# Mixture weights loaded in one head and parted in the next, every other head from 7 to 42

## The chip, the core and the metric

The kernel runs on one core of a Trainium2 chip. The core has five engines with instruction queues of their own: PE (TensorE, matrix products), DVE (VectorE), ACT (ScalarE), POOL (GpSimd) and SP (SyncE, which here issues nearly all the DMAs). [...] The metric is the device time of one execution in microseconds (us), lower is better, as the median of several runs.

## The reference, cut to what matters

One transformer block over 4 sequences of 512 tokens, 256 wide, all in float32: causal attention with 16 heads, and then a mixture of 8 experts of which each token uses two.

```python
mod = (_silu(c) @ wmod).reshape(B, 6, 1, -1)
sa, ca, ga, sb, cb, gb = (mod[:, i] for i in range(6))
...
h = _layernorm(x) * (1 + ca) + sa
x = x + ga * attention(h, W_K, W_Q, W_V, W_O)
h = _layernorm(x) * (1 + cb) + sb
x = x + gb * mixture(h, ...)
```

```python
# mixture, x being h above
h = x @ down_w + down_b
gate, topi = softmax_of_top_2(softmax(x @ router_w + router_b - COST_LAMBDA * cost))
for k in range(2):
    mask = one_hot(topi[..., k], 8)
    for e, (w1, b1, w2, b2) in enumerate(expert_params):
        hm = h * mask[..., e:e + 1]
        acc = acc + (gelu(gelu(hm) @ w1 + b1) @ w2 + b2)
    out = out + acc * gate[..., k:k + 1]
out = out + 0.1 * (gelu(gelu(h) @ shared_w1 + shared_b1) @ shared_w2 + shared_b2)
out = out @ up_w + up_b + gelu(x) @ core_w + core_b
```

The experts' hidden widths are 128, 256, 384, 512, twice. The change concerns the weights of this mixture, but its instructions run in the middle of the attention.

## The kernel before, in words

**Products in three parts.** To keep float32 accuracy at a fast matmul, most operands are *parted*: `hi` is the operand cast to `float32r`, `lo` is what is left (`full - hi`), and a product is three matmuls (`mm3`, lines 139 to 141). Activations are parted as they come out of PSUM: a cast on ACT and a subtraction (`rest`, line 147).

**Mixture weights are parted early and kept in DRAM.** `UNITS` cuts the mixture's weights into units of up to four blocks of 128 columns. Eleven are to be parted, in this order (`TO_PART`): first0 to first4, second0 to second2, shared, core, down; all have 128x512 elements but shared and down, which have 128x256. `part_wf` (line 218) does one unit:

- load the unit from `wf` into a `stage` tile `st_wf` (line 181, one DMA for each run of adjacent blocks, so one to three),
- for the second units, write the whole unit to DRAM (line 225),
- cast it to `hi_wf` on ACT, which takes another `stage` tile (line 227), and write that to DRAM (line 228),
- subtract on POOL, in place in `st_wf` (line 147), and write that to DRAM (line 230).

There are two buffers of the tag `stage`. They are also used by `load_unit` (line 184) for the attention's weights `wqk`, `wv`, `wo`, and by `route`. The parted units come back from DRAM with `load_wf` and `load_parts` near the end of the attention.

**The loop over heads.** The attention runs over 64 heads, numbered n = 0 to 63 (four groups of four heads, in each group the four sequences). One turn of the loop holds, for head n: the scores `ps` in four tiles t = 0 to 3 (line 475 for t = 0, `mm3` for the others), a reduction on DVE that leaves the scores in `e` and their least in `nmax` (line 481), the exponential on ACT (line 491), the reciprocal of the sum on DVE (line 495) and the scaling on POOL (line 496). Between them stand the projections `pq` and `pk` of head n + 1 and half of the values `pv` of a pair of heads. Then `turned` transposes `e` in blocks on DVE into `T` (lines 505 and 511), writes `T` to DRAM in four DMAs (`moved`, line 517) and reads it back as `aT` (line 521). `parted` casts `aT` on ACT to `aTh` (line 528) and subtracts on POOL. Three heads later `mixed` multiplies it with the values into `pz`, which ACT casts into `zh` (line 546) and DVE parts into `zl`, and one turn later `project_out` multiplies that with `wo` into `po`. The tiles `e`, `T`, `aTh` and the PSUM tile of the scores have two buffers each, `aT` three.

**What sets the order.** TensorE's instructions stay in the order of the code (`manual_schedule`). Those of the other engines and of SP are put in order by the framework's planner[...]. [...] Some attention weights must wait: the tag `wu` has ten buffers, so that in each group the loads from the second `wqk` of head 12 (28, 44) on wait for weights to fall out of use.

`PART_AT` (line 101) lists the heads in whose turn a unit is parted; lines 1042 and 1043 call `part_wf` there, ahead of the projections of that turn:

```python
PART_AT = (17, 19, *range(20, 28), 33)
...
        if n in PART_AT:
            part_wf(TO_PART[PART_AT.index(n)])
```

## Time and profile before

| | |
|---|---|
| median of 3 runs | 824.99 us (823.43 to 825.74) |
| the profiled execution | 824.06 us |
| its span | 822.3 us |
| TensorE busy | 777.1 us (95%), mean granted clock 0.988 |
| VectorE busy | 597.4 us (73%) |
| ScalarE busy | 490.4 us (60%) |
| GpSimd busy | 521.4 us (63%) |
| DMA moved | 124.12 MB, mean 151 GB/s |
| attention on TensorE, from the first score of head 0 to that of head 63 | 19.73 to 625.63 us |

The profile is of one execution. An engine's busy time is the sum of its instructions; waiting is not in it. In the timeline each line has a start, a length, the engine, the line of the kernel, the operation, out<-in with tile names, and in brackets how long the engine had been idle before it and what released it. A matmul's end is modelled. SPq is the DMA-issuing queue: its records show the issue, not the transfer; from issue to landing a load of 256 KB takes between 3 and 4 us in the median (`st_wqk` 3.8, `st_wv` 3.4), the 160 KB of one `moved` 2.8 and the 640 KB of an `aT` 3.9 us.

### The profile page before, as it was taken

How to read it: one execution, taken by the hardware profiler on the slowest of the kernel's cores; microseconds unless marked ns; L12 is line 12 of the kernel's file. 1: busy time of each engine (PE TensorE's matmuls, PEld its weight loads, DVE VectorE, ACT ScalarE, POOL GpSimd, SP SyncE). 2: the span in 40 equal slices, each digit the busy share in tenths (PEclk: the TensorE clock that was granted, in tenths of full speed). 3: DMA queues.
4: the chain of work that ended last, by engine and by line, in shares of the span. 5: the costliest groups of instructions: out<-in, count | busy, mean ns of one | idle time of the engine just before them, and what ended most of it. 6: DMA issues, size and time to landing. Idle time of an engine off the chain costs nothing. (4 is left out here: it accounts for less than half of the span.)

```text
span 822.3 us, 14105 instructions
## 1 busy us (share of the span) xinstructions
PE 777.1 (95%) x4487; PEld 671.3 (82%) x4487; DVE 597.4 (73%) x1734; ACT 490.4 (60%) x1184; POOL 521.4 (63%) x523
## 2 busy tenths in 40 slices
PE   6889999999998799999999999999998898989997
PEld 5678989999887689999999999999887775767775
DVE  5968787776655676767777776779898577795555
ACT  3556666566656656666666656665667343656663
POOL 4645566886756568866556895656565346564675
PEclk9999999999999999999999999999999899999999
DMA  7365354666676746665454665554566332222221
GB/s 235 113 182 156 111 151 128 198 174 204 200 212 198 218 151 183 188 179 161 128 156 133 198 168 162 165 157 138 155 182 216 104 120 86 94 62 68 61 81 61
DMA packets 73218, 124.12 MB, mean 151 GB/s; under 512 B 8996, under 2 KB 51252, under 8 KB 73144
## 3 DMA queue, kind: packets, MB, share of 16 engines
q1 hardware_dynamic: 73112, 123.21, 51.1%
q8 instruction: 36, 0.59, 0.3%
q14 instruction: 38, 0.31, 0.1%
q0 software_dynamic: 32, 0.02, 0.0%
HBM read 73.05 MB, written 50.14 MB: 150 GB/s over the span
## 5 line engine op out<-in xcount | busy, mean ns | idle before, releaser
L147 POOL TENSOR_TENSOR aT<-aT,aTh 128x1152 fp32r<-128x1152 f32 x64 | 171.9, 2687 | 127.1 <-ACT aTh L528 124.2
L496 POOL TENSOR_SCALAR e<-e,inv 128x128 f32<-128x128 f32 (+3 forms) x256 | 135.7, 543 | 66.8 <-DVE inv L495 64.8
L491 ACT ACTIVATE e<-e,nmax 128x128 f32<-128x128 f32 (+3 forms) x256 | 143.4, 562 | 45.9 <-DVE nmax L481 44.8
L528 ACT CAST aTh<-aT 128x1152 fp32r<-128x1152 f32 x64 | 74.0, 1156 | 127.4 <-DMA aT<-moved 64.5
L481 DVE CUSTOM_DVE_ANT_0 e<-ps,mask 128x128 f32<-128x128 f32 (+3 forms) x256 | 120.9, 479 | 31.0 <-PE ps L475 19.7
L511 DVE STREAM_TRANSPOSE T<-e 128x384 f32<-128x384 f32 (+2 forms) x256 | 100.4, 445 | 9.8 <-POOL e L496 9.7
L139 PE MATMUL ps<-kh,ql 128*128 128x256 f32 (+2 forms) x192 | 72.0, 375 | 17.1 <-DVE nmax L481 17.1
L147 DVE TENSOR_TENSOR zl<-pz,zh 128x512 fp32r<-128x512 f32 x64 | 44.0, 687 | 56.9 <-ACT zh L546 56.3
L139 PE MATMUL po<-wo,zl 128*128 128x256 f32 x256 | 73.3, 286 | 4.5 <-DVE zl L147 4.2
L140 PE MATMUL po<-wo,zh 128*128 128x256 f32 x256 | 72.0, 281 | 0.0
L141 PE MATMUL po<-wo,zh 128*128 128x256 f32 x256 | 72.0, 281 | 0.0
L139 PE MATMUL pv<-wv,hTl 128*128 128x256 f32 x256 | 71.7, 280 | 0.0
L140 PE MATMUL pv<-wv,hTh 128*128 128x256 f32 x256 | 71.5, 279 | 0.0
L141 PE MATMUL pv<-wv,hTh 128*128 128x256 f32 x256 | 71.5, 279 | 0.0
L856 POOL TENSOR_TENSOR oacc<-oacc,part 128x512 f32<-128x512 f32 x28 | 40.9, 1462 | 43.4 <-DVE part L852 36.8
L495 DVE RECIPROCAL inv<-tot 128x1 f32<-128x1 f32 x256 | 40.0, 157 | 36.5 <-ACT e L491 29.6
L139 PE MATMUL pz<-aTh,vl 128*128 128x512 f32 (+2 forms) x192 | 65.5, 341 | 0.0
L140 PE MATMUL pz<-aT,vh 128*128 128x512 f32 (+2 forms) x192 | 65.3, 340 | 0.0
L140 PE MATMUL ps<-kl,qh 128*128 128x256 f32 (+2 forms) x192 | 65.2, 339 | 0.2 <-DVE kl L147 0.2
L141 PE MATMUL pz<-aTh,vh 128*128 128x512 f32 (+2 forms) x192 | 65.3, 340 | 0.0
L141 PE MATMUL ps<-kh,qh 128*128 128x256 f32 (+2 forms) x192 | 64.9, 338 | 0.0
L139 PEld LDWEIGHTS ps<-kh,ql 128*128 128x128 f32 x192 | 36.6, 191 | 28.0 <-DVE nmax L481 19.9
(216 smaller groups left out, 2331.2 us busy)
## 6 DMA issues: line engine op xcount, KB each, us to landing
moved<-T SPq DMA_DIRECT2D x256, 160.0 KB, 2.8
aT<-moved SPq DMA_DIRECT2D x64, 640.0 KB, 3.9
spread<-gates_e SPq DMA_DIRECT2D x32, 256.0 KB, 3.2
st_wqk<-in_wqk SPq DMA_DIRECT2D x16, 256.0 KB, 3.8
wf_first<-wfp_first SPq DMA_DIRECT2D x5, 512.0 KB, 5.9
st_wv<-in_wv SPq DMA_DIRECT2D x8, 256.0 KB, 3.4
st_wo<-in_wo SPq DMA_DIRECT2D x8, 256.0 KB, 3.7
wmod<-in_wmod SPq DMA_DIRECT2D x6, 256.0 KB, 5.2
```

The lines of the kernel that those rows point to most:

```text
L139: nc.tensor.matmul(o, lhsT=wl, rhs=mh, start=start, stop=False)
L140: nc.tensor.matmul(o, lhsT=wh, rhs=ml, start=False, stop=False)
L141: nc.tensor.matmul(o, lhsT=wh, rhs=mh, start=False, stop=stop)
L147: return eng.tensor_tensor(lo, full, f32(hi), ALU.subtract)
L481: least = nc.vector.tensor_tensor_reduce(out=et, in0=ps[:, :n], in1=maskf[:, S - n :], scale=-SCALE, scalar=BIG, op0=ALU.add, op1=ALU.min, ...
L491: exp = nc.scalar.activation(et, et, AF.Exp, bias=nm[:, t : t + 1], scale=-1.0, accum_out=tot[:, t : t + 1])
L495: nc.vector.reciprocal(inv[:, one], tot[:, one])
L496: by_sum = nc.gpsimd.tensor_scalar(et, et, inv[:, one], 1.0, ALU.mult, ALU.mult)
L511: nc.vector.transpose(to[:, first : first + n], blocks[:, at : at + (n - 1) * step + 1 : step])
L528: nc.scalar.copy(hi, full)
L856: recent["added"] = nc.gpsimd.tensor_tensor(oacc, oacc, to, ALU.add).ins
```

## The change

The load is taken out of `part_wf` into a function of its own, `stage_wf`, which is called one head ahead of `part_wf`; and the eleven heads are others: 7, 9, 11, then 20, 22, 24, 26, then 36, 38, 40, 42. The order of the units is the same. The loads are thus called in heads 6, 8, 10, 19, 21, 23, 25, 35, 37, 39 and 41.

```diff
-PART_AT = (17, 19, *range(20, 28), 33)
+PART_AT = (7, 9, 11, 20, 22, 24, 26, 36, 38, 40, 42)
...
+    staged: dict[str, bass.AP] = {}
+
+    def stage_wf(u: str):
+        n = len(UNITS[u][0]) * P
+        staged[u] = work.tile([P, 512], F32, tag="stage", name=f"st_wf_{u}")[:, :n]
+        load_runs(staged[u], wf_runs(u))
+
     def part_wf(u: str):
 
         n = len(UNITS[u][0]) * P
-        st = work.tile([P, 512], F32, tag="stage", name=f"st_wf_{u}")[:, :n]
-        load_runs(st, wf_runs(u))
+        st = staged[u]
         d = parts_d[u] = dram.tile([P, 3, n], F32, tag=f"wfp_{u}", name=f"wfp_{u}")
         if u.startswith("second"):
             nc.sync.dma_start(d[:, 2, :], st)
...
         for f, *args in later.pop(n, ()):
             f(*args)
+        if n + 1 in PART_AT:
+            stage_wf(TO_PART[PART_AT.index(n + 1)])
         if n in PART_AT:
             part_wf(TO_PART[PART_AT.index(n)])
```

## The prediction, made before the changed kernel was run

> **What bounds the kernel now.** The order of reading was: the page's busy table and its 40 slices, then the same in windows cut at heads, then who waits for whom in the bad stretch, then the timeline there. TensorE is busy 777.1 of 822.3 us, so the question is where the other 45 us lie. In the page's slices (20.6 us each) these two rows answer it:

> ```profile
> PE   6889999999998799999999999999998898989997
> ...
> PEclk9999999999999999999999999999999899999999
> ```

> Outside the start, the attention half (slices 0 to 30) has one hole, slices 11 to 13. A head begins on TensorE with its first score product (line 475); the timeline has these at 137.58 (head 12), 211.10 (head 20) and 309.10 (head 29). Heads 12 to 19 take 9.19 us each, and so do the heads from 29 on. Heads 20 to 28 take 98.00 us where nine of 9.19 us are 82.7: **15.3 us are lost there**, and since everything behind moves at TensorE's pace, they are lost to the end. The windows of heads 7, 21, 23 and 26 (columns: from and to, length, then busy us of PE, PEld, DVE, ACT, POOL with counts, clock, DMA share, GB/s):

> ```profile
> 90.60:99.78 9.18, 9.18 (x60) 8.38 (x59) 7.30 (x23) 5.81 (x15) 6.06 (x6) 1.00 0.53 145
> ...
> 220.54:231.53 10.99, 9.44 (x61) 8.31 (x59) 6.04 (x21) 7.12 (x19) 6.62 (x6) 1.00 0.66 215
> ...
> 241.63:254.78 13.15, 9.72 (x60) 8.38 (x59) 6.02 (x22) 6.44 (x17) 5.99 (x7) 1.00 0.69 201
> ...
> 276.98:289.58 12.60, 9.45 (x60) 8.31 (x59) 8.72 (x28) 7.78 (x20) 6.69 (x7) 1.00 0.69 226
> ```

> No engine is full in the long heads (ACT 6 to 8 us of 11 to 13); something waits. The waits between 205 and 300 us name it (us in total, times, longest):

> ```profile
> ACT hi_wf_second L227 <- DMA st_wf_second<-in_wf: 11.2, 2, 6.0
> ...
> ACT hi_wf_first L227 <- DMA st_wf_first<-in_wf: 5.1, 2, 2.6
> ACT hi_wf_shared L227 <- DMA st_wf_shared<-in_wf: 3.7, 1, 3.7
> ...
> ACT hi_wf_core L227 <- DMA st_wf_core<-in_wf: 2.2, 1, 2.2
> ```

> That is 22.2 us in which ScalarE stood before the cast of a mixture unit whose load had not landed. The timeline around 248 us shows how it reaches TensorE:

> ```profile
> 243.49 1.44 SPq L181 DMA_DIRECT2D st_wf_second<-in_wf  x3
> ...
> 248.50 0.33 SPq L225 DMA_DIRECT2D wfp_second<-st_wf_second  x1
> 248.53 0.62 ACT L227 CAST hi_wf_second<-st_wf_second 128x512 fp32r<-128x512 f32 x1 [5.98 <-DMA st_wf_second<-in_wf]
> ...
> 248.87 2.20 SPq L517 DMA_DIRECT2D moved<-T  x4
> 249.05 1.15 ACT L528 CAST aTh<-aT 128x1152 fp32r<-128x1152 f32 x1
> ...
> 250.72 0.69 DVE L147 TENSOR_TENSOR zl<-pz,zh 128x512 fp32r<-128x512 f32 x1 [5.46 <-ACT zh L546]
> ...
> 251.46 0.39 PE L139 MATMUL po<-wo,zl 128*128 128x256 f32 x1 [2.23 <-DVE zl L147]
> ```

> Two queues stand: ScalarE behind the cast (aTh, zh and the exponentials are late, then VectorE, then TensorE), and SP behind line 225, which waits for the same load, so that `moved` is issued late and with it the next `aT`. With one unit in every head the loads leave SP at 231.56, 243.49, 254.97 and 266.55: a loop of some 11.6 us in a head of 9.19.

> [...] `moved` leaves at 248.87, right behind line 225. [...] here three issues took 1.44 us and their landing 4.3 us median. [...] heads 2 and 3 (35.55 to 57.31) ran at a clock of 0.84 and 0.85, with 128x512 matmuls of 0.63 us instead of 0.39.

> **The change, part by part.** Nothing is added or removed: the eleven units keep their loads, casts (0.62 us, 0.41 for two blocks), subtractions on POOL (1.29, 0.75) and writes; TensorE's list is instruction for instruction the same, and the other engines' lists have the same lengths. What moves is read from the order of each engine's instructions in both programs. The planner lifts work ahead as buffers allow, so the places are not those of the code. Before: first0 and first1 are cast at the starts of heads 17 and 19, then eight units follow in heads 19 to 25, one or more per head, then down at head 33. After, three groups:
> - A: first0, first1, first2 in heads 2, 3 and 4 (the code says 7, 9, 11).
> - B: first3 at the start of head 19, first4, second0, second1 at the ends of heads 19, 20, 21.
> - C: second2 at the start of head 35, shared, core, down up to the start of head 37.

> *Removed, the run of eight: 15.3 us.* Head 28 (10.33 us) counts as its tail, since head 12, of the same kind, takes 9.19. When this stall goes, nothing else is late there: TensorE itself needs the 9.19 us, so no more than 15.3 can be had.

> *B.* first3 stands as first1 did, loaded two heads ahead: nothing (first1's cast at 205.25 waited for nothing). first4 stands as first2 did, whose ScalarE wait of 2.48 us cost head 20 only 0.25 us. second0: SP issues its load behind `moved` of head 19, at about 217 instead of 231.6, and `aT` goes out between the load and line 225, so the landing (4.3 us) overlaps work that has to wait anyway; ScalarE, there at about 219, waits until about 221.5, 2.5 us. But the cast now stands behind vh of its head, not ahead of it as first3's did at 221.16, where vl (2.97 us) and the 1.55 us of TensorE at 224.22 followed. second1's load leaves at about 225.5 and lands by 230; ScalarE gets there at about 230.5. So 0.25 + some 1 + some 0.75: **2 us**. Low end 0.5 (first4 alone costs); high end 5.7, three times the mean of the old run (15.3/8 = 1.9).

> *C.* second2 is loaded two heads ahead: nothing. shared stands as first2 did. core's load waits on SP for a stage buffer ahead of `moved` of head 35, so that and its `aT` leave 1 to 2 us later than in B. down stands as down did before, which cost nothing (head 33 took 9.19). **1.5 us**; low 0, high 4 (two units at 1.9).

> *A.* On SP the load of first0 stands behind `moved` of head 0, at 36.7; a load issued at 36.77 landed in 3.9, so 40.6. ScalarE is at the cast at 38.4 and waits 2.2 us. The load of first1 goes half behind `moved` of head 1, which itself comes 1.6 us later (behind first0's writes and the four gate rows): landing about 51.5, ScalarE there at 50.6, wait 0.9. first2: landing about 59.3, ScalarE there at 58.1, wait 1.2. These 4.3 us have cover, because in this stretch ScalarE waits for `aT` in each head:

> ```profile
> 44.75 1.16 ACT L528 CAST aTh<-aT 128x1152 fp32r<-128x1152 f32 x1 [2.18 <-DMA aT<-moved]
> ...
> 61.59 1.16 ACT L528 CAST aTh<-aT 128x1152 fp32r<-128x1152 f32 x1 [3.50 <-DMA aT<-moved]
> ```

> On POOL 3 x 1.29 us stand ahead of softmax scalings, and POOL is busy 2.76 and 6.76 us of heads 2 and 3. VectorE's list puts the transposes of heads 1, 3 and 4 behind a score reduction they preceded, which takes away waits like the 1.48 us of TensorE at 60.91. Taken at **0.5 us**. From below: a gain of 1.5. From above: all 4.3 us uncovered plus one more half-clock window (3.4 us long, as the two at 38.5 and 48.5, so 1.7 lost): 6.

> Sum: 15.3 - 2 - 1.5 - 0.5 = 11.3 us. The profiled execution took 824.06 us (span 822.3): 812.8. The median of the three runs is 0.9 above that execution, which gives 813.7; I say **813 us**.

> **The rivals.**
> - *The stall is only moved.* The planner leaves groups B and C one unit per head, so the change isn't the spacing it says. If each of their six close units costs the old 1.9 us, 11.5 come back: gain 3.8, less 0.5, **821**. For it: casts still follow their load closely in SP's list. Against: the loss grew along the old run (0.25, 1.8, 0.9, 4.0 us in heads 20 to 23), and runs of three end before it grows.
> - *No change.* Groups B and C at their high ends (9.7) and A near its own (6): **824.5**. Against: three independent groups would all have to go badly.
> - *The start pays: slower.* Heads 2 to 4[...] half clock holds from 37 to 68 us, 31 us lose 15.5, of which 3.4 (two windows) are lost already: 12.1, and 4.3 of waits: 16.4. Net 16.4 + 3.5 - 15.3 = 4.6 slower, **829**. It decides from a loss of 11.8 us in the start. For it: the clock of 0.84. Against: [...] the cover above.

> **How the numbers follow.** Forecast 0.73; moved stall 0.13; no change 0.05; start pays 0.09. A measurement of this kernel can tell 0.3% (2.5 us) from nothing. Faster: 0.73 + 0.13 = 0.86; within: 0.05; slower: 0.09. The forecast's own ends are 807.8 (all low ends: 15.3 + 1.5 - 0.5 = 16.3 off 824.06) and about 819 (half of what the high ends are above the values taken: 5.9 more). The range 808.5 to 820.5 leaves out the last corner below, the two worst cases and part of the moved stall.

> **What would show it.** Right: no head from 23 to 28 above 9.5 us, the start of head 29 at about 296 to 300, casts of second0 and second1 waiting under 3 us each, heads 35 to 38 within 2 us of 36.8. The start: head 7 at about 90.6, within 1.5. Wrong: head 7 later than 96, or waits on `st_wf` of over 10 us in groups B and C, or heads above 11 us there.

## The result, and the profile after

The changed kernel takes **815.59 us** (median of 4 runs, 814.61 to 818.48) beside 825.10 for the kernel before (four runs). The ratio is put at 0.9903, 95% interval 0.9875 to 0.9932, which is a gain of 8.0 us (5.6 to 10.3); it isn't the quotient of the two medians, 0.9885. The forecast was 813, in a range of 808.5 to 820.5. The profiled execution of the changed kernel took 815.89 us, with a span of 814.1; the one before took 824.06 and 822.3.

The two rows of the page that showed the hole, now of the kernel after (40 slices of 20.4 us, busy share in tenths):

```profile
PE   6898999999999999999999999999998998989997
...
PEclk9999999999999999999999999999999899999999
```

Slices 12 and 13, which were 8 and 7, are at 9. What is left is too small for this view, so heads are measured as before, from one first score product (now line 482) to the next. Windows of four heads of the kernel after, 3, 21, 22 and 23 (columns: from and to, length, busy us of PE, PEld, DVE, ACT, POOL with counts, clock, DMA share, GB/s):

```profile
46.88:54.77 7.89, 7.89 (x48) 6.91 (x47) 5.92 (x21) 4.77 (x16) 4.33 (x7) 1.00 0.77 245
...
220.81:229.99 9.18, 9.18 (x60) 8.38 (x59) 4.76 (x19) 5.50 (x15) 5.30 (x5) 1.00 0.87 257
229.99:240.81 10.82, 9.63 (x60) 8.39 (x59) 5.60 (x20) 6.00 (x16) 5.40 (x5) 1.00 0.69 218
240.81:252.33 11.52, 9.97 (x61) 8.47 (x59) 9.10 (x28) 7.13 (x19) 6.84 (x9) 1.00 0.65 195
```

Heads 21 and 26, which took 10.99 and 12.60, are at the 9.19 that TensorE needs. Heads 22 and 23 are not. A ledger from such starts, in us over the floor of 9.19 for each head where that floor holds:

| stretch | before | after |
|---|---|---|
| head 0 to head 7 (group A; length) | 70.87 | 70.87 |
| heads 20 to 28 (group B), over 82.7 | 15.3 | 4.0 |
| heads 37, 38, 40 (group C), over 27.6 | 0 | 3.25 |

15.3 - 4.0 - 3.25 is 8.05. Head 0 starts 0.5 us later (20.23 beside 19.73), so that head 63 starts 7.56 us earlier (618.07 beside 625.63); the end is 0.6 us shorter still, which makes the 8.2 us between the spans.

The waits between 205 and 300 us in the kernel after (us in total, times, longest):

```profile
POOL st_wf_second L148 <- DMA wfp_second<-st_wf_second: 8.8, 2, 4.5
...
ACT hi_wf_second L234 <- DMA st_wf_second<-in_wf: 5.5, 2, 3.0
...
ACT hi_wf_first L234 <- DMA st_wf_first<-in_wf: 3.1, 1, 3.1
```

8.6 us are left there of the 22.2 that ScalarE spent ahead of such casts. Shared and core are now cast behind this window and cost ScalarE another 4.03 and 1.84 us, so 14.5 us remain in groups B and C. POOL's line is new: it subtracts in place, and both times it started only when the write of the whole unit (now line 232), which reads the same buffer, had landed: at second1 the write landed at 235.94, and POOL began at 236.11 after 4.53 us of waiting. The timeline of the kernel after shows the last cast of B, second1's:

```profile
226.28 1.13 SPq L182 DMA_DIRECT2D st_wf_second<-in_wf  x2
...
228.59 0.33 SPq L528 DMA_DIRECT2D aT<-moved  x1
...
228.96 0.43 SPq L182 DMA_DIRECT2D st_wf_second<-in_wf  x1
...
233.64 0.62 ACT L234 CAST hi_wf_second<-st_wf_second 128x512 fp32r<-128x512 f32 x1 [2.57 <-DMA st_wf_second<-in_wf]
...
234.65 3.17 SPq L524 DMA_DIRECT2D moved<-T  x4
```

The unit is loaded in three pieces, and the planner has put the third behind the `aT` of that head, so it leaves 2.7 us after the first two and lands, with the 640 KB of `aT` under way, at about 233.5. ScalarE was free at about 231. SP's writes at lines 232 (233.61) and 235 (234.28) wait for the same landing and for the cast, and hold `moved` until 234.65. In the head that follows, TensorE stood 1.11 us at 245.01 for a score reduction. The chain of work that ended last, followed back from there (start, length, what), goes through several queues:

```profile
221.64 0.62 ACT hi_wf_second L234
...
224.31 4.17 DMA moved<-T
...
228.96 4.58 DMA st_wf_second<-in_wf
...
233.61 2.33 DMA wfp_second<-st_wf_second
...
236.11 1.29 POOL st_wf_second L148
237.40 2.66 POOL aT L148
...
245.01 0.45 PE ps L140
```

second0's landing releases its cast on ScalarE, behind which SP's `moved`, `aT` and the third piece of second1 leave late. From that piece's landing on, the chain runs over the whole unit's write and POOL's subtraction, with POOL's `aT` part and the softmax scaling behind it. ScalarE's wait is thus one of several ways from a late landing to TensorE; at second1 POOL's ended last. The wait of 5.98 us shown before had a next one 11.5 us later, and this one has none: after two such heads the stall ends.

In group C a cast again stands right behind its load. Timeline of the kernel after, at shared and core:

```profile
359.90 0.37 SPq L182 DMA_DIRECT2D st_wf_shared<-in_wf  x1
...
364.27 0.41 ACT L234 CAST hi_wf_shared<-st_wf_shared 128x256 fp32r<-128x256 f32 x1 [4.03 <-DMA st_wf_shared<-in_wf]
...
364.70 0.32 SPq L235 DMA_DIRECT2D wfp_shared<-hi_wf_shared  x1
...
366.50 0.33 SPq L182 DMA_DIRECT2D st_wf_core<-in_wf  x1
366.87 2.15 SPq L524 DMA_DIRECT2D moved<-T  x4
```

A load that was called a head earlier in the code is still followed by its cast at once: 4.03 us of waiting here. SP stands at line 235 for that cast (until 364.70), at line 237 for the subtraction (until 365.51), and then 0.6 us for a stage buffer for core; so `moved`, whose last block VectorE had turned by 363.68, leaves at 366.87, 3.2 us later.

### The profile page after: what moved, and what is told of

Read it like the earlier page. It is cut to its first block, busy times and chain, and to the rows that moved or that the text cites. A ratio compares the mean times of both kernels' runs of the same rounds, so it can differ in the third digit from the quotient of the medians.

```text
span 814.1 us, 14111 instructions
## 1 busy us (share of the span) xinstructions
PE 776.6 (95%) x4487; PEld 671.2 (82%) x4487; DVE 596.6 (73%) x1734; ACT 490.1 (60%) x1184; POOL 520.6 (64%) x523
## 4 chain that ended last, share of the span: by engine, by line
PE 72%; DVE 10%; DMA 7%; POOL 4%; ACT 2%; issue 2%; SPq 2%; DVEq 0%; ACTq 0%; POOLq 0%
PE acc L835 4%; PE ps L140 3%; PE pz L140 3%; PE pz L141 3%; PE pz L142 3%; PE ps L141 3%; PE ps L142 3%; PE po L140 3%; PE po L141 3%; PE po L142 3%; PE pk L141 3%; PE pk L140 3%; PE pk L142 3%; PE pv L140 3%; PE pv L142 3%; PE pv L141 3%
## 5 line engine op out<-in xcount | busy, mean ns | idle before, releaser
L140 PEld LDWEIGHTS ps<-kh,ql 128*128 128x128 f32 x192 | 36.5, 190 | 22.3 <-DVE nmax L488 15.3
```

What stands on the lines that cost most here:

```text
L140: nc.tensor.matmul(o, lhsT=wl, rhs=mh, start=start, stop=False)
```

## The experiments

**The theory** that came out of these traces: the loss is made by *lateness*. The planner puts a cast on ScalarE right behind its load (first0's, called in head 7 of the changed kernel, ran at 40.46, in head 2), so ScalarE waits for the landing (5.98 us at the longest, in which its records show no other work) with aTh, zh and the exponentials behind. One such wait is mostly absorbed (first2's 2.48 us cost head 20 0.25), close ones are not. **The rival**: it is *density*. Several units in a row load SP, the DMA engines, ScalarE and POOL so much that heads grow, however punctual the casts. A third: the wait that counts is *SP's*, at the second units' whole write ahead of `moved`. POOL's wait for that write was not among the theories; the runs on SP's wait meet it.

All times are medians; heads and waits are those of one profiled execution of each. Each version ran beside the kernel before, whose median was 824.8 us, or 825.57 (for 811.45, 816.37, 817.65 and 811.86) or 826.38 (for 820.57). The ratios, again, aren't quotients of these medians.

### Lateness or density: the old heads with the casts held back

`issue_after` is given `exp1`, the second exponential, on ScalarE, of the head in which the code calls `part_wf`. In the trace of this kernel the second unit's cast stands right behind that exponential (issued at 244.14, the cast at 244.63), while its load (238.51) and its whole write (243.58) still go ahead of it; so of `part_wf` only the cast is held. The units stay in the heads of before, one per head.

```diff
-        _, least, *_ = next(scores)
+        _, least, exp1, *_ = next(scores)
...
         if n in PART_AT:
-            part_wf(TO_PART[PART_AT.index(n)])
+            with tc.issue_after(exp1):
+                part_wf(TO_PART[PART_AT.index(n)])
```

> The kernel before, with its old heads (17, 19, 20 to 27, 33) and without the split of load and parting, but each unit's cast on ScalarE is put behind the second exponential of the head that the code names, so that it can't be lifted up to its load. The units stay one per head. Theory 1 (the loss is ScalarE standing before a load that has not landed; how dense the units are does not matter): the 15.3 us of heads 20 to 28 nearly go, heads at 9.2 to 9.6 us, 809 to 813 us. Theory 2 (SP's queue can't carry one unit per head beside moved and aT, a loop of 11.6 us): the heads stay above 10 us, 818 us or more. Theory 3 (DMA traffic itself): as theory 2.

Measured: **813.36 us** (811.97 to 816.53), ratio 0.984 (0.9792 to 0.9888). Heads 20 to 28 take 87.5 us, 4.8 over their floor instead of 15.3. Its timeline at the first second unit:

```profile
243.58 0.34 SPq L225 DMA_DIRECT2D wfp_second<-st_wf_second  x1
244.63 0.60 ACT L227 CAST hi_wf_second<-st_wf_second 128x512 fp32r<-128x512 f32 x1
```

The load left at 238.51 and the cast runs at 244.63, with no bracket: ScalarE did not wait for it. Eight close units are still there, and two thirds of their cost are gone (10.5 of 15.3 us). Lateness is most of it. 4.8 us stay, in heads 24 and 26 to 28. What ScalarE waits for now is `aT`: 21.5 us in seven waits between 205 and 300 us, where it was 9.8 in four. The longest, and what follows from it:

```profile
263.15 0.33 SPq L225 DMA_DIRECT2D wfp_second<-st_wf_second  x1
...
268.71 0.34 SPq L521 DMA_DIRECT2D aT<-moved  x1
...
273.44 1.16 ACT L528 CAST aTh<-aT 128x1152 fp32r<-128x1152 f32 x1 [5.00 <-DMA aT<-moved]
...
282.30 0.44 PE L139 MATMUL ps<-kh,ql 128*128 128x384 f32 x1 [1.02 <-DVE nmax L481]
```

SP stood at line 225 for second2's landing, `moved` left at 263.52 and `aT` behind it; the chain that ended last runs from this `aT` to the wait of TensorE at 282.30. That is the third theory's wait, on SP. How much of the 4.8 us it makes in all isn't known.

### SP's wait alone

The whole write of a second unit is copied from `wf` in DRAM instead of from the stage buffer, so SP has nothing to wait for there.

```diff
         if u.startswith("second"):
-            nc.sync.dma_start(d[:, 2, :], st)
+            load_runs(d[:, 2, :], wf_runs(u))
```

> The kernel before, but the unparted copy of the three second units (line 225) is made from DRAM to DRAM, so that SP no longer waits there for the load into the stage tile; casts, loads and subtractions stay. Theory 1 (ScalarE's queue): the casts still wait, gain under 3 us, 822 to 825 us. Theory 2 (SP's queue): heads 22 to 24 lose 4 to 6 us less, 819 to 821 us.

Measured: **822.76 us** (819.42 to 824.51), ratio 0.9966 (0.9948 to 0.9984). Heads 20 to 28 take 96.96 us, 14.3 over the floor: one of the 15.3 us. ScalarE's waits on the second units got shorter (second1 3.84, before 5.98; second2 3.89, before 5.19), those on first2 and first3 a little longer (2.82 and 2.79, before 2.48 and 2.58). This run also touches the start, where head 0 to head 7 take 71.96 us instead of 70.87; but with the casts still late, taking away the wait at line 225 gives back almost nothing.

### The heads alone, without the split

The kernel before with nothing changed but `PART_AT`; load and cast stay in one function.

```diff
-PART_AT = (17, 19, *range(20, 28), 33)
+PART_AT = (7, 9, 11, 20, 22, 24, 26, 36, 38, 40, 42)
```

> The kernel before with the new heads 7 to 42 alone; load and parting stay in one function, called in one head. The planner lifts the loads in either case, and the lists of all engines come out as in the changed kernel. Expected: the changed kernel's time, 815.6 within 1.5 us. If the split by a head does something of its own, 818 us or more.

Measured: **817.65 us** (814.89 to 818.27), ratio 0.9892 (0.9859 to 0.9925), which can't be told from the change's 0.9903. The median lies 0.6 us above the range expected, and the order of instructions decides: it is the same on every engine as in the changed kernel; heads 20 to 28 take 86.1 us here (86.68 there), and heads 37, 38 and 40 lose 3.7 (3.25). So half of the change in words, "loaded in one head and parted in the next", does nothing by itself: the planner puts the loads at the same places in either form. The other half alone, the split with the old close heads, wasn't tried: with two stage buffers, two staged units leave none for the cast.

### The new heads with the casts held

In the changed kernel, held as above, first for all units:

```diff
         if n in PART_AT:
-            part_wf(TO_PART[PART_AT.index(n)])
+            with tc.issue_after(exp1):
+                part_wf(TO_PART[PART_AT.index(n)])
```

> The changed kernel with each cast put behind the second exponential of the head that the code names (7, 9, 11, 20 to 26, 36 to 42, every other). Theory 1: groups B and C cost nothing more (4.0 and 3.2 us in the changed kernel's profile), and heads 2 to 6 go back to what they took before; 824.9 - 15.3 = 809 to 811 us. Theory 2: B and C lose at least half of what they lose in the changed kernel, 812 us or more.

Measured: **814.61 us** (810.99 to 815.45), ratio 0.9842 (0.9802 to 0.9883). The 809 to 811 of theory 1 was missed. Group B loses 3.2 us and C 0.5, and the start takes 68.97 us instead of 70.87. But head 10 grows from 10.25 to 14.69. Its timeline there:

```profile
115.27 2.67 SPq L182 DMA_DIRECT2D st_wf_first<-in_wf  x2
117.99 2.50 SPq L524 DMA_DIRECT2D moved<-T  x4
119.79 1.15 ACT L535 CAST aTh<-aT 128x1152 fp32r<-128x1152 f32 x1 [5.80 <-DMA aT<-moved]
...
123.72 0.69 PE L390 MATMUL ptn<-ident,xn 128*128 128x128 f32 x4 [2.84 <-DVE hTl L148]
```

Two loads of first2 took 2.67 us to issue, with `moved` behind them, and the `aT` before them, issued at 114.28, was waited for until 119.79, 5.5 us (3.9 from issue to landing in the median before): ScalarE waits 5.80, TensorE 2.84, and the matmuls after it run at half clock (0.88 over the head; a 128x512 matmul takes 0.63 us instead of 0.39). Head 10 also turns a new normalized input `xn` (line 390), takes 10.25 us even undisturbed, and has no room. Against this, lifting A's units to heads 2 to 4 was no loss.

Then for groups B and C alone, `if n > 11`:

> The changed kernel with the casts of groups B and C held at their heads as in the run before, those of group A left where the planner lifts them (heads 2 to 4). Against that run it shows what group A costs in the start. My prediction had 0.5 us: within 1 us of the run with all casts held, 809 to 811 us. If the start pays (the third rival), 2 us or more above it.

Measured: **812.02 us** (811.58 to 812.63), ratio 0.982 (0.9786 to 0.9854), below the change's interval. It is neither within 1 us of the run before nor slower than it, as the two expectations had it, but 2.6 us faster, since head 10 stays at 10.24. All heads of C are at 9.18 or 9.19, and so are heads 20 to 25; B loses 2.7 us, in heads 26 to 28. So holding the casts gives the changed kernel 3.6 us between the medians and 4.3 between the profiled executions, of the 7.25 in the ledger. It also spreads them: shared, core and down are cast at 383.50, 401.65 and 419.06 us, every second head, and at 364.27, 369.47 and 378.32 in the changed kernel. Lateness and closeness go away together here; only the old heads separate them. What is left in B, by the timeline of this kernel:

```profile
256.49 1.39 SPq L182 DMA_DIRECT2D st_wf_second<-in_wf  x3
...
261.98 0.33 SPq L232 DMA_DIRECT2D wfp_second<-st_wf_second  x1
...
266.99 0.34 SPq L528 DMA_DIRECT2D aT<-moved  x1
...
271.00 1.15 ACT L535 CAST aTh<-aT 128x1152 fp32r<-128x1152 f32 x1 [3.85 <-DMA aT<-moved]
```

SP waits for second1's landing (until 5.5 us after the issue began) ahead of `moved` (262.35), so `aT` leaves late and ScalarE waits 3.85 us for it; with the casts on time, the third theory has a case of its own.

### SP's wait, with the casts on time

The write is held on SP behind the `aT` read that the code has last called, that of the head before; `recent["aT"]` keeps its instruction.

```diff
         if u.startswith("second"):
-            nc.sync.dma_start(d[:, 2, :], st)
+            with tc.issue_after(recent["aT"]):
+                nc.sync.dma_start(d[:, 2, :], st)
```

On top of the kernel with B and C held:

> Run e4 (changed kernel, casts of groups B and C held at their heads) with one more edit: the unparted copy of a second unit is issued on SP behind the read of aT, not right behind its own load, where SP stood 5 us before moved could leave (261.98 in e4). The two together are theory 1 and what was right in theory 2. Expected: the 2.5 us that heads 26 and 27 still lost in e4 go, 809 to 810.5 us. If those come from DMA traffic instead (theory 3), no change: 811.5 to 812.5.

Measured: **811.45 us** (810.9 to 812.28), ratio 0.9824 (0.9789 to 0.9858). Heads 20 to 28 take 83.99 us, 1.3 over the floor instead of 2.7. The heads agree with the theory; the medians, 0.6 us apart, can't decide.

On top of the kernel before with its casts held:

> Run e1 (kernel before, units one per head, casts held) with the same edit of SP's order. If lateness on the two queues is all of the 15.3 us, heads 20 to 28 take under 84.5 us in all and the time is 809 to 811. If units one per head also cost by their traffic, more than 3 us of the 4.8 that e1 still lost stay: 812 or more.

Measured: **816.37 us** (813.79 to 818.28), ratio 0.9881 (0.9845 to 0.9917). Heads 20 to 28 lose 7.1 us, where they lost 4.8 without this edit. By the letter that is the second expectation, but not for its reason, traffic. The timeline of this kernel in head 26, which took 13.64:

```profile
265.92 1.37 SPq L181 DMA_DIRECT2D st_wf_second<-in_wf  x3
...
269.89 0.62 ACT L228 CAST hi_wf_second<-st_wf_second 128x512 fp32r<-128x512 f32 x1 [2.35 <-DMA st_wf_second<-in_wf]
...
274.13 0.69 PE L139 MATMUL ps<-kh,ql 128*128 128x384 f32 x1 [2.67 <-DVE nmax L482]
274.14 0.32 SPq L231 DMA_DIRECT2D wfp_second<-st_wf_second  x1
274.51 2.24 SPq L518 DMA_DIRECT2D moved<-T  x4
```

A write that is held keeps its stage buffer, so the next unit's load comes late (second2's at 265.92; without the edit it left at 258.65) and its cast, held or not, stands right behind the landing again: 2.35 us. And another write of the unit, line 231, now stands ahead of `moved` in the place of the first. The wait was passed on, not taken away.

The same edit on the changed kernel, with nothing held on ScalarE:

> The changed kernel with one thing changed: the whole write of a second unit stands on SP behind the aT of the part_wf's own turn (heads 22, 24, 26 ... of the code), so SP never waits at it ahead of moved; nothing is held on ScalarE. The write keeps its stage buffer that much longer, so the third unit of group B (second1) is loaded and cast some three heads later than before, and second0 stands alone. Theory (a cast right behind its load stalls ScalarE, and the stall reaches TensorE only when a second one follows in the next head): first4 and second0 still wait some 3 us each on ScalarE; heads 22 and 23, which took 10.82 and 11.52, come down to 9.2 to 9.5, one later head with second1 may take up to 10.5, the shared-core-down group still loses 3 to 4 us; 20 to 29 loses 1 to 2 us instead of 4.0; total about 813. Rival (SP's wait ahead of moved is what carries the stall to TensorE): no head from 20 to 29 above 9.3, the other group unchanged, about 811.5. Second rival (the close units cost the same wherever they stand): total 815 to 816, the 4 us only found in other heads.

Measured: **820.57 us** (819.22 to 820.85), ratio 0.9927 (0.9902 to 0.9952). A miss for all three expectations. Its fastest run is above the slowest of the changed kernel, though the intervals of the ratios overlap. Heads 20 to 29 lose 5.6 us and heads 38 to 41 lose 4.4; another 1.8 us are lost in the start, where TensorE's clock halved in head 5 (last section). Windows of this kernel for heads 22 and 24, and its timeline afterwards:

```profile
231.14:241.17 10.03, 9.46 (x61) 8.32 (x60) 8.32 (x26) 6.22 (x17) 5.43 (x6) 1.00 0.35 82
...
250.35:260.85 10.50, 9.46 (x61) 8.32 (x60) 9.06 (x28) 5.96 (x16) 7.74 (x8) 1.00 0.48 118
```

```profile
257.92 0.43 SPq L233 DMA_DIRECT2D wfp_second<-st_wf_second  x1
...
262.76 1.30 POOL L148 TENSOR_TENSOR st_wf_second<-st_wf_second,hi_wf_second 128x512 fp32r<-128x512 f32 x1 [3.78 <-DMA aT<-moved]
```

The write at 257.92 reads the buffer in which POOL is to subtract in place, so POOL waits 3.78 us, with its own `aT` part and the softmax scalings behind. (The releaser in the bracket is inferred; the write landed 4.7 us after its issue, just ahead of the subtraction.) The changed kernel has this wait at second0 and second1, so the run moved SP's wait without taking POOL's away and doesn't isolate either. Heads 22 and 24, though, lose 0.8 and 1.3 us while no cast, load or subtraction of a unit runs (between 223 and 257 us), at a DMA share of 0.35 and 0.48. Why they lose was not settled. The waits of aTh for `aT` don't tell: they sum to 20.9 us between 205 and 300 here, and to 20.0 in the version that takes 812.02.

### Group A elsewhere

The same as the version of 811.45, with A's heads 4, 6 and 8 instead of 7, 9 and 11 and their casts held too:

```diff
-PART_AT = (7, 9, 11, 20, 22, 24, 26, 36, 38, 40, 42)
+PART_AT = (4, 6, 8, 20, 22, 24, 26, 36, 38, 40, 42)
```

> Run e5 with the three units of group A held in heads 4, 6 and 8 instead of being lifted to 2, 3 and 4. In e3, with them held in 7, 9 and 11, the start was 2.1 us faster up to head 7, but head 10, in which a norm is modulated, took 14.7 us. Expected: head 7 begins at 88.5 to 90 us, head 10 stays at 10.24, 807 to 809.5 us. If the start needs the lifted places, 811 or more.

Measured: **811.86 us** (809.97 to 813.21), ratio 0.9827 (0.9794 to 0.9859). The start takes 69.1 us, as expected, but head 10 takes 12.09 (10.25): what the start gains is given back, and the 807 to 809.5 was missed. With 811.45 and 812.02 it makes three versions that cannot be told apart, some 4 us below the changed kernel and 13 to 14 below the one before.

## Why the prediction was right, point by point

- **The run of eight, 15.3 us: right.** Heads 24 to 28 are at 9.18 to 9.22 after the change, and nothing else was late behind the stall.
- **Group B, 2 us: measured 4.0.** Head 29 starts at 298.30, inside the 296 to 300 named; but "no head from 23 to 28 above 9.5" fails for head 23 (11.52). The waits of second0 and second1 were 2.97 and 2.57, under 3 as said. The mis-sized terms are the last two of the sum, some 1 and some 0.75 for second0 and second1. second1 was to land by 230 and not to be waited for; its third piece left at 228.96, behind `aT`, and landed at about 233.5. The prediction took the load's first issue and a plain landing time, and didn't look at which piece came last; nor does it have POOL's wait for the whole unit's write, over which the chain into head 23 runs.
- **Group C, 1.5 us: measured 3.25.** Heads 35 to 38 take 39.18, 2.4 over 36.8 where 2 were allowed. Shared was to wait 2.48 like first2 and waited 4.03, and core 1.84. `moved` was to leave 1 to 2 us late for core's stage buffer; that buffer cost 0.6 of the 3.2 us measured; the rest are shared's late cast, its subtraction and its writes ahead of `moved` on SP. The version with held casts takes this whole cost away, but it also spreads the casts to every second head, so it doesn't say whether lateness or closeness made it.
- **Group A, 0.5 us: measured 0.0**, head 7 at 91.10 where about 90.6 was said. ScalarE stood 1.74, 1.50 and 1.85 us before the three casts, where 2.2, 0.9 and 1.2 were said. But the balance has large terms: head 3 takes 7.89 (11.18 before), its half-clock stretch gone (clock 1.00, 0.85 before), and head 5 12.85 (10.50 before). That they cancel was not forecast and is luck. Nor is 0.0 exact to better than 1 us: where the start's instruction lists are those of before, head 0 to head 7 took 70.87, 71.65 and 73.15 us in three profiles, and where they are those of after, between 70.27 and 72.70 in five.
- **The sum:** 11.3 us forecast; 8.2 in the profiled executions, 9.5 between the medians, and 8.0 by the ratio, whose interval (5.6 to 10.3) leaves the 11.3 out. The miss is in B and C, 3.75 us together, and the range was wide enough for it.
- **The signs.** Of the three signs of being wrong that the prediction named, two came: a head above 11 us in group B (head 23), and waits before the casts of B and C of over 10 us, if they are added up (14.5). So the direction and the removed stall were right, and the account of what comes back was not.
- **The rivals.** *The stall is only moved* priced a close unit at 1.9 us, the forecast at about 0.6 (3.5 us for six). The six close units of B and C cost 7.25, so 1.2 each: halfway between, and this rival names rightly what is left. *The start pays* didn't come: the clock over head 3 rose to 1.00. That longer waits of TensorE would halve its clock was the author's guess; in head 5 of the changed kernel a wait of 3.41 us left it at 1.00. Lateness and density, which the prediction held together in "a loop of some 11.6 us", came apart only in the runs: the old heads with the casts held take 813.36, and the new heads with B and C held 812.02. Spacing by itself is worth little once the casts are on time.

What stays open: how much of the 4.8 us that eight close and punctual units still cost is SP's wait; how the changed kernel's loss in B divides between ScalarE, SP and POOL; and the heads that lose without a unit in them.

## What to carry to other kernels

When a planner lifts an instruction to just behind its own load, as it did here with the cast before which ScalarE stood 5.98 us, look at the order that it emits and at the piece of the load that leaves last, not at where the code calls it; holding the consumer back in the old heads was worth at least as much here (11.4 us between the medians) as the change of heads (9.5). Before a wait is moved off one queue, list what else holds the buffer it keeps: here the next load and an in-place subtraction, and the stall was found again on ScalarE and on POOL. Freed time at the start was worth nothing here: with all casts held the start took 68.97 us instead of 70.87, but head 10, ahead of which first2's loads now left, took 14.69 instead of 10.25.

## What the runs showed of the hardware

```profile
66.29:69.71 3.42, 1.52 (x8) 0.91 (x6) 0.92 (x4) 1.07 (x4) 3.16 (x5) 1.00 0.77 232
69.71:73.12 3.41, 1.91 (x9) 1.69 (x10) 3.41 (x11) 1.51 (x6) 0.78 (x2) 1.00 0.62 196
...
68.35:71.76 3.41, 0.30 (x2) 0.30 (x3) 2.50 (x9) 0.26 (x1) 2.29 (x3) 1.00 0.58 145
71.76:75.18 3.42, 3.42 (x10) 2.86 (x9) 3.10 (x10) 2.43 (x8) 0.60 (x2) 0.50 0.49 179
```

In head 5 of the changed kernel TensorE waits 3.41 us for a score reduction (until 71.21). The pause lies across two steps, counted on from 42.40; TensorE is busy 1.52 and 1.91 us in them, and the clock stays at 1.00. In the version of 820.57 the same wait is shorter, 3.23 us (until 71.46), but in the 3.41 us ahead of the half clock TensorE is busy only 0.30 us; the next 3.41 run at 0.50, with 128x512 matmuls of 0.63 us, which take 0.39 or 0.40 behind them. With all casts held a pause of 2.84 us (until 123.72) does the same: the 128x512 matmuls at 124.63 and 125.06 take 0.63 us, and the 128x256 ones 0.41 or 0.42 up to 127.19 and 0.28 from 127.61 on.

The idle time in a step doesn't settle it either: in the kernel before, the step from 45.20 to 48.61 has TensorE busy for 1.90 us and is followed by half clock, as is the step from 35.58 to 38.99 in the changed kernel, with 1.88; the two steps of 1.52 and 1.91 above are not. And the waits ahead of the half clock in heads 2 and 3 of the kernel before, 1.52 and 1.22, and 1.49 us, are all shorter than the 3.41 that left the clock at 1.00. What does decide was not shown.
